# Two rounds of graph layers: when a gather may start, and how the node numbers are multiplied

## The chip, the cores and the metric

The kernel runs on one core of a Trainium2 chip. The metric is the device time of one launch in microseconds (us). Before the change it is 2184.74 us, the median of 9 runs (2181.94 to 2186.77).

## The reference, cut to what matters

Two graph layers run one after the other over the same 6,250 nodes of 256 numbers and 106,250 edges (100,000 edges and a loop at each node), which come sorted by target node.

```python
# layer 0: a message network of one of two kinds on every edge, then a cell and three products a node
S = feat[src]
for r in range(2):
    msgs = where(rel == r, edge_nn(S, W_rel[r], b_rel[r]), msgs)
agg = segment_sum(msgs, dst, n_nodes)
gates = agg @ W_ih.T + b_ih + b_hh            # i, f, g, o
hn = sigmoid(o) * tanh(sigmoid(i) * tanh(g))
x = layernorm(x + mlp3(hn))
# layer 1: attention with 4 heads of 64
h = (x @ W).reshape(n, 4, 64)
e = leaky_relu(a_src[src] + a_dst[dst], 0.2)  # one logit an edge and head
ex = exp(e - segment_max(e, dst)[dst])
out = segment_sum(h[src] * ex / segment_sum(ex, dst)[dst], dst)
x = layernorm(x + relu(layernorm(out + x) * gamma + beta))
```

## The kernel before, in words

The edges are cut into 782 tiles of 128 (`TC`), seven tiles make a window (`WT`), two windows a group; there are 56 groups (`NG`) in pairs, the last four alone. The kernel runs in four stretches.

**Start, to about 212 us.** The edge list is packed, and TensorE makes both kinds of message for all nodes (L1557, L1571) and stores them as table `parts`. Sixty gathers of the first layer (L1605) are issued in it already; the list `soon` holds their tiles.

**First aggregation, about 212 to 1160 us.** A loop over n from 60 to 785 is written out by hand. Step n issues one gather of 128 message rows from the table by an indirect DMA of the POOL queue (L1717), and adds the tile that was gathered four steps earlier (`LAG`) to its group's sum on TensorE (L2175, `sum0`). For every four finished groups a chain `update` is started, which a small hand scheduler (`Steps`) moves on a little at each step: gates (L2006), small products (L2030 to L2054), norm, turn (L2079), product with the attention weights (L2092), store of the new rows. For the first 12 windows the 60 early tiles are summed by extra chains (`sums_ahead`).

**Second aggregation, about 1160 to 2133 us.** Step t issues the gather of 128 rows of the new table (L1717, the same helper line). Four steps later its logits count as landed; when the last tile of a window counts as landed, ScalarE copies that window's logits out of the rows (L2626), and at the first tile of the next group that tile's logits (L2618). Then `weights` makes the weights of a whole pair (L2378 to L2409), `weighted` multiplies the rows by them on VectorE (L2424 to L2430), and `sum1` sums them on TensorE (L2546). `finish` ends a group. Meanwhile `ahead` brings, for a later pair, the slot of each edge's target within its group: it loads 15 tiles' slots, the same for all 128 partitions, as `dB` (L2313), compares them with the partition number to a one-hot `ohT` (L2338) and multiplies it with the group's node numbers `node3` (L2345). The `dB` tile has one buffer.

**End, 2133 to 2183.6 us.** The last weights, sums and norms, without gathers.

The gathers of both aggregations land in a ring of ten windows' buffers. On the POOL queue they stand one behind the other. What holds a gather back is its buffer, the landing of the gather eight before it, and a tie that `Pace.hold` adds: `passes` notes at the end of each step the last VectorE instruction issued so far, and gather n waits for the one noted `ahead` steps earlier. `AHEAD0` is 14 in the first aggregation; in the second it is `AHEAD1` = 8 and a surplus that falls from 42 to 0 over 252 steps and rises again over the last 42.

Three classes of tiles within a group matter for the change: tiles 0 to 6 of a group point at its lower 64 node slots, tiles 10 to 14 at its upper 64, tiles 7 to 9 at all 128 (`MID` = 7, 10; `LOW` = 64; `GS` = 15).

Of the kernel before, what the change touches and what calls it, by code (L numbers as in the profile page):

```python
# [38 lines left out]
ET = mybir.EngineType  # L39
# [3 lines left out]
P = 128  # L43
N = 6250
D = 256
E = 106250
H = 4
# [18 lines left out]
WT = 7  # L66
# [18 lines left out]
AHEAD_G = range(AHEAD_W // 2)  # L85
LATE = 3
CR = 16 * WT
AHEAD0 = 2 * WT
AHEAD1 = WT + 1
NOROW = NP + P // 2 - 1  # L90
SORTED = "the fast path runs only where the chip has found the edges sorted"

# [1547 lines left out]
def fast(  # L1640
# [46 lines left out]
    def at(ap, offset, dims):  # L1687
        return bass.AP(tensor=ap.tensor, offset=ap.offset + offset, ap=dims)
# [35 lines left out]
    class Steps:  # L1724
# [18 lines left out]
        def finish(self):  # L1743
            while self.chains:
                self.step()

    class Pace:
# [4 lines left out]

        def passes(self):
            traced = nc.cur_bb.bb.instructions
            self.passed.append(next(i for i in reversed(traced) if i.engine == ET.DVE))

        def hold(self, move, n, ahead):
            n -= self.first + ahead
            if n < 0:
                return  # L1760
            tc.add_manual_dep(
                move.ins,
                self.passed[n].name,
                mybir.DependencyInfo(mybir.DependencyClass.Sync, mybir.DependencyReason.DATA),
                reason="rows come no sooner than they are wanted",
            )
# [489 lines left out]
    with (  # L2256
# [45 lines left out]
        def ahead(pair, box):  # L2302

            cut = ring(ep, [P, P + 1], F32, "cut", 3)
            of = ring(ep, [P, 2 * GS, 2 * H], F32, "of", 3)
            box.update(cut=cut, of=of)
            i0, n = pair[0] % 2, len(pair)
            if i0 == 0:
                box["dB"] = ring(ep, [P, 2, GS * P], BF16, "dB", 1)
            else:  # L2310
                box["dB"] = boxes[pair[0] - 1]["dB"]
            dB = box["dB"][:, i0 : i0 + n, :]
            nc.sync.dma_start(  # L2313
                dB.rearrange("p i e -> p (i e)"),
                at(slots, pair[0] * GS * P, [[0, P], [1, n * GS * P]]),
            )
            if pair in pairs[:2]:
                for i, g in enumerate(pair):
                    nc.sync.dma_start(
                        cut[i * GS * H : (i + 1) * GS * H, :],  # L2320
                        at(cuts, tiles_in(g)[0][0] * P, [[P, GS], [0, H], [1, P + 1]]),
                    )
            else:
                o = pair[0] % 2 * GS * H
                n = ((len(pair) - 1) * GS + len(tiles_in(pair[-1])[1])) * H
                pc = ring(tps, [P, P + 1], F32, "turn", 2)
                nc.tensor.matmul(
                    pc[:n, :],
                    pick[:, pair[0] % 8 // 2, o : o + n],
                    cut_all[:, pair[0] // 8, :],  # L2330
                    start=True,
                    stop=True,
                )
                nc.scalar.copy(cut[:n, :], pc[:n, :])
            yield 12 if len(pair) > 1 else 8
            for i, g in enumerate(pair):
                ohT = ring(ep, [P, GS, P], BF16, "ohT", 2)
                nc.vector.tensor_scalar(  # L2338
                    ohT.rearrange("p j e -> p (j e)"), dB[:, i, :], iota_p, None, op0=OP.is_equal
                )  # L2340
                yield 2
                n = len(tiles_in(g)[1])
                pn = ring(ops, [P, GS, 3, 2 * H], F32, "pn", 2)
                for j in range(n):
                    nc.tensor.matmul(  # L2345
                        pn[:, j, :, :].rearrange("p c a -> p (c a)"),
                        ohT[:, j, :],
                        node3[:, g, :, :].rearrange("p c a -> p (c a)"),
                        start=True,
                        stop=True,  # L2350
                    )
                    if j == WT:
                        yield 1
                yield 1
                nc.vector.tensor_reduce(
                    of[:, i * GS : i * GS + n, :],
                    pn[:, :n, :, :].rearrange("p j c a -> p j a c"),
                    axis=AX.X,
                    op=OP.add,
                )  # L2360
                yield 1
# [56 lines left out]
        def weighted(g, w, o, n, of, ex, top):  # L2418

            if g not in ohs:  # L2420
                ohs[g] = ring(ep, [P, (2 * WT - 2) * LOW + 3 * P], F32, "oh1", 2)
                one_hot(ohs[g], g, slot, MID[1])
            gw = ring(ep, [P, WT if n > 1 else 1, D + 2 * H], F32, f"gw{min(n, 2)}", 4)[:, :n, :]
            nc.vector.tensor_mul(  # L2424
                gw[:, :, HA:],
                top[:, o : o + n, :],
                first[:, WT * w : WT * w + n, None].to_broadcast([P, n, H]),
            )
            nc.scalar.copy(gw[:, :, D:HA], ex[:, o : o + n, :])  # L2429
            nc.vector.tensor_mul(  # L2430
                gw[:, :, :D].rearrange("p j (h f) -> p j h f", h=H),
                of[:, :n, :D].rearrange("p j (h f) -> p j h f", h=H),
                ex[:, o : o + n, :, None].to_broadcast([P, n, H, F]),
            )
            return gw

        def finish(g, ps):
# [76 lines left out]
        results = {}  # L2514

        def sum1():

            while late and len(queue) < 8:
                piece = late.pop(0)
                g, w, o, n = piece[:4]  # L2520
                gw = weighted(*piece)
                queue.extend((g, WT * w + j, gw[:, j, :]) for j in range(n))
            if not queue:
                return
            g, t, gw = queue[0]
            if g not in sums and g >= 2 and g - 2 not in read:
                return
            queue.pop(0)
            if g not in sums:
                sums[g] = ring(eps, [P, D + 2 * H], F32, "fps1", 2)  # L2530
                left[g] = len(tiles_in(g)[1])
                u = everyone
                if g % 2 == 0:
                    k3s[g // 2] = ring(fp, [P, 2, 3, D], F32, "k3", 2)
                of = k3s[g // 2].rearrange("p i c f -> p i (c f)")
                if len(pair_of[g]) == 1:
                    nc.sync.dma_start(of[:, g % 2, :], kept[g // 2, :, g % 2, :])
                elif g % 2 == 0:
                    nc.sync.dma_start(of, kept[g // 2])
            begins = left[g] == len(tiles_in(g)[1])  # L2540
            left[g] -= 1
            j = t - 2 * WT * g
            to, cols = place(j, MID[1])
            ohj = ohs[g][:, cols]
            ends = left[g] == 0 or j in (WT - 1, TC - 1 - 2 * WT * g)
            nc.tensor.matmul(sums[g][to, :], ohj, gw, start=begins, stop=ends)  # L2546
            if left[g] == 0:
                run.start(finish(g, sums[g]), 1)

        def aheads():  # L2550
            for pair in pairs:
# [42 lines left out]
        while t < TC + LAG or late or queue or run.chains:  # L2594
            if EARLY <= t < TC:
                w = t // WT
                if t % WT == 0:
                    G[w] = ring(rowsp, [P, WT * HA], F32, "G", 10).rearrange(
                        "p (j f) -> p j f", f=HA
                    )  # L2600
                move = gather(G[w][:, t - WT * w, :], rows1, idx1[:, t : t + 1])
                pace.hold(move, t, AHEAD1 + max(0, 6 * WT - (t - EARLY) // 6, 3 * WT - (TC - t) // 2))
            k = t - LAG
            if 0 <= k < TC:
# [6 lines left out]
                if k % (2 * WT) == 0:  # L2611
                    if g == pair[0]:
                        box["e"] = ring(ep, [P, 2 * GS, H], F32, "e", 3)
                    if g:
# [5 lines left out]
                        )  # L2620
                        if old is not pair:
                            run.start(weights(old, ob))
                if k == tiles_of(w)[0][-1]:
                    o = pair.index(g) * GS + WT * (w % 2)
                    own = len(tiles_of(w)[0])
                    nc.scalar.copy(box["e"][:, o : o + own, :], G[w][:, :own, D:HA])  # L2626
                    if w == NW - 1:
                        run.start(weights(pair, box))
            sum1()
# [67 lines left out]
```

## Time and profile before

| what | value |
|---|---|
| median of 9 runs | 2184.74 us (2181.94 to 2186.77) |
| profiled execution | 2185.4 us, span 2183.6 us |
| granted TensorE clock, mean | 0.839 |
| busy: PE, DVE, ACT, POOL | 73%, 60%, 23%, 71% |
| gathers of both aggregations on POOL (L1717) | 722, 21 early ones of the second, 761 |
| DMA queues | POOL's 33.7% of 16 engines' span, SP's 17.6% |

PE is TensorE, DVE VectorE, ACT ScalarE, POOL GpSimd, SP the queue that issues most plain DMAs. The span is the time from the first to the last recorded instruction; 1.8 us of the profiled execution lie around it. A row of the timeline view gives start, duration, engine, line, operation, output<-input, and in brackets the idle time before it with what ended that. Lines are those of the kernel before.

### The profile page before, as it was taken

To read this page: it belongs to the slowest core of one execution; us is meant where nothing else is said; L and a number is where in the kernel's file an instruction comes from. 1 tells how busy PE (TensorE), PEld (TensorE's weight loads), DVE (VectorE), ACT (ScalarE), POOL (GpSimd) and SP (SyncE) were. 2 spreads that over 40 slices of the span, in tenths; PEclk is the share of its full clock that TensorE was granted. 3 is DMA by queue.
4 is the path that set the end of the run, shared out by engine and by line. 5 is a ranking of instruction groups with operands and counts; after the bars stand their busy time and mean duration, and the time that the engine had idled before them with its cause. 6 is when DMAs were issued, how large, how long until landed. Compare 5 with 4: busy or idle time off the path is not lost.

```text
span 2183.6 us, 23269 instructions
## 1 busy us (share of the span) xinstructions
PE 1588.6 (73%) x6390; PEld 851.8 (39%) x6390; DVE 1320.0 (60%) x3622; ACT 498.7 (23%) x1538; POOL 1548.9 (71%) x1610
## 2 busy tenths in 40 slices
PE   8988998788888898888995656565565556555564
PEld 5656544333333343333554333233232333333332
DVE  7854344434333433434443788888877777878786
ACT  3333032122211222122342121221211112121112
POOL 2465677777777777777777777777777777777770
PEclk9999999999989989999997777676776767677776
DMA  5356645445554555445555555555555555554551
GB/s 158 113 170 175 187 147 185 145 141 171 167 161 127 165 167 166 131 154 172 184 156 166 173 177 161 165 168 159 178 164 159 164 159 164 159 173 150 171 153 37
DMA packets 146105, 346.12 MB, mean 159 GB/s; under 512 B 36154, under 2 KB 66720, under 8 KB 145965
## 3 DMA queue, kind: packets, MB, share of 16 engines
q0 software_dynamic: 76048, 207.99, 33.7%
q1 hardware_dynamic: 67741, 133.51, 17.6%
q10 hardware_dynamic: 2176, 3.05, 0.4%
q8 instruction: 52, 0.85, 0.2%
q14 instruction: 88, 0.72, 0.1%
HBM read 291.90 MB, written 52.52 MB: 158 GB/s over the span
## 4 chain that ended last, share of the span: by engine, by line
PE 29%; DVE 23%; DMA 17%; issue 11%; POOL 7%; ACT 5%; DVEq 0%; SPq 0%; ACTq 0%; POOLq 0%
PE fps L2175 11%; DMA G<-parts,fidx 8%; DMA G<-rows,fidx 8%; POOL G L1717 7%; DVE gw L2430 6%; PE fpg L2006 5%; PE fps L2546 4%; DVE oh L1832 4%; PE fpg L2092 2%; PE fps L2288 1%; PE fpm L1571 1%; DVE fst L2476 1%; ACT fy L2484 1%; PE fpg L2054 1%; DVE ohT L2338 1%
## 5 line engine op out<-in xcount | busy, mean ns | idle before, releaser
L1717 POOL DMA_INDIRECT G<-rows,fidx x761 | 732.7, 963 | 232.0 <-issue 132.0
L1717 POOL DMA_INDIRECT G<-parts,fidx x722 | 694.3, 962 | 231.1 <-issue 154.0
L2546 PE MATMUL fps<-gw,oh 128*64 128x264 f32 (+1 forms) x1674 | 465.3, 466 | 187.9 <-DVE gw L2430 187.9
L2175 PE MATMUL fps<-G,oh 128*64 128x257 f32 (+1 forms) x1674 | 501.8, 418 | 114.9 <-DMA G<-parts,fidx 101.2
L2546 PEld LDWEIGHTS fps<-gw,oh 128*64 128x64 f32 (+1 forms) x1674 | 240.3, 176 | 332.9 <-DVE gw L2430 202.5
L2175 PEld LDWEIGHTS fps<-G,oh 128*64 128x64 f32 (+1 forms) x1674 | 210.2, 156 | 382.1 <-DMA G<-parts,fidx 181.7
L2430 DVE TENSOR_TENSOR gw<-G,bank 128x1792 f32<-128x1792 f32 (+1 forms) x167 | 249.0, 1491 | 58.0 <-ACT gw L2429 57.9
L2006 PE MATMUL fpg<-faT,fWihT 128*128 128x512 f32 (+2 forms) x432 | 171.7, 522 | 0.0
L1832 DVE TENSOR_TENSOR oh<-bank,fslot 128x448 f32<-128x448 f32 (+2 forms) x318 | 156.6, 548 | 9.4 <-ACT bank L2409 6.6
L1924 DVE TENSOR_SCALAR kind<-fps 128x1 f32<-128x1 f32 x112 | 12.5, 153 | 213.5 <-PE fps L2175 213.5
L1571 PE MATMUL fpm<-fWrT,fhT 128*128 128x256 f32 x392 | 96.5, 400 | 14.0 <-DVE fms L1579 14.0
L2126 DVE COPY nd<-hr 128x4 f32<-128x4 f32 x53 | 10.0, 189 | 156.0 <-ACT hr L2098 156.0
L2006 PEld LDWEIGHTS fpg<-faT,fWihT 128*128 128x128 f32 x432 | 72.1, 193 | 67.1 <-issue 56.2
L1557 PE MATMUL fph<-fxc,fWrT 128*128 128x512 f32 (+1 forms) x208 | 89.9, 582 | 4.8 <-DMA fWrT<-in_WrT_dram 4.8
L1605 POOL DMA_INDIRECT G<-parts,fidx x60 | 62.2, 1036 | 42.0 <-DVE fms L1579 18.0
L1571 PEld LDWEIGHTS fpm<-fWrT,fhT 128*128 128x128 f32 x392 | 76.9, 200 | 32.7 <-DVE fms L1579 11.2
L2345 PE MATMUL pn<-node,ohT 128*128 128x24 bf16 x837 | 41.0, 180 | 66.2 <-DVE ohT L2338 66.2
L2484 ACT ACTIVATE fy<-fy,frs 128x256 f32<-128x256 f32 x112 | 66.9, 597 | 87.3 <-DVE frs L2481 87.0
L2478 ACT ACTIVATE frs<-fmv,eps_c 128x1 f32<-128x1 f32 x112 | 32.9, 294 | 228.6 <-DVE gw L2424 150.8
L2378 PE MATMUL turn<-fident,e 128*120 128x128 f32 (+2 forms) x30 | 11.8, 393 | 98.3 <-ACT e L2618 98.3
L2092 PE MATMUL fpg<-Wx,fyT 128*128 128x264 f32 x224 | 74.8, 463 | 3.0 <-ACT fyT L2083 3.0
L2345 PEld LDWEIGHTS <-ohT 128*128 128x128 bf16 x837 | 34.2, 103 | 107.2 <-DVE ohT L2338 74.1
(348 smaller groups left out, 1970.1 us busy)
## 6 DMA issues: line engine op xcount, KB each, us to landing
dB<-slots SPq DMA_DIRECT2D x26, 960.0 KB, 5.5
kept<-keep SPq DMA_DIRECT2D x26, 768.0 KB, 4.6
k<-kept SPq DMA_DIRECT2D x26, 768.0 KB
loop<-parts SPq DMA_DIRECT2D x55, 256.0 KB, 2.8
parts<-fms SPq DMA_DIRECT2D x49, 256.0 KB, 2.6
G<-parts,fidx POOLq DMA_INDIRECT x782
G<-rows,fidx POOLq DMA_INDIRECT x761
out_dram<-fy SPq DMA_DIRECT2D x56, 128.0 KB, 1.9
```

Of the source, the lines that this page charges most:

```text
L1557: nc.tensor.matmul(ph[:, :cols], WrT_s[:, r, k, m * P : (m + 1) * P], xc[:, k, :cols], start=(k == 0), stop=(k == 1),)
L1571: made = nc.tensor.matmul(pm[:, r, :], hT[:, r, k, j * P : (j + 1) * P], WrT_s[:, r, k, :], start=(k == 0), stop=(k == 1),)
L1605: nc.gpsimd.indirect_dma_start(out=of[:, n % WT, :D], out_offset=None, in_=parts0[: 2 * P * block, :], in_offset=bass.IndirectOffsetOnAxis ...
L1717: return nc.gpsimd.indirect_dma_start(out=to_tile, out_offset=None, in_=table, in_offset=bass.IndirectOffsetOnAxis(ap=idx, axis=0),)
L1832: nc.vector.tensor_tensor(to[:, o : o + len(js) * n].rearrange("p (j s) -> p j s", s=n), iota_s[:, None, cols].to_broadcast([P, len(js), n ...
L2006: nc.tensor.matmul(pg[:, :cols], WihT_s[:, k, c * P : (c + 1) * P], aT[:, k, :cols], start=(k == 0), stop=(k == 1),)
L2092: nc.tensor.matmul(ph[u, :], hs[i][:, k, u], Wx[:, k, :], start=(k == 0), stop=(k == 1))
L2175: nc.tensor.matmul(sums[g][to, :], ohj, got[t], start=begins, stop=ends)
L2345: nc.tensor.matmul(pn[:, j, :, :].rearrange("p c a -> p (c a)"), ohT[:, j, :], node3[:, g, :, :].rearrange("p c a -> p (c a)"), start=True ...
L2430: nc.vector.tensor_mul(gw[:, :, :D].rearrange("p j (h f) -> p j h f", h=H), of[:, :n, :D].rearrange("p j (h f) -> p j h f", h=H), ex[:, o ...
L2484: nc.scalar.activation(y, y, AF.Identity, bias=m, scale=r)
L2546: nc.tensor.matmul(sums[g][to, :], ohj, gw, start=begins, stop=ends)
```

## The change

Ties: a gather is now held only where its number divides by four (`EVERY`), so one wait stands ahead of four gathers; it is 6 steps back in the first aggregation and 4 (with the same surplus) in the second, in place of 14 and 8; and what is noted at the end of a step is TensorE's last instruction, not VectorE's.

Node-number products: a tile of the lower half and one of the upper half now share one product. The slots of tile j are loaded to the lower 64 partitions and those of tile j+10 to the upper 64, so `dB` and `ohT` have 10 tiles in place of 15; the node numbers are put by two ScalarE copies into `node2`, whose two halves hold the lower and the upper nodes and zeros elsewhere; 10 products replace 15. Three DMAs replace one. Five memsets are added once.

Logit copies: the copies of a group's two windows are made together, when its second window counts as landed.

The product of rows and weights (L2430) no longer waits for the gathers of its rows, since its weights come from their logits.

```diff
-AHEAD0 = 2 * WT
-AHEAD1 = WT + 1
+AHEAD0 = WT - 1
+AHEAD1 = WT - 3
+EVERY = 4
...
-            self.passed.append(next(i for i in reversed(traced) if i.engine == ET.DVE))
+            self.passed.append(next(i for i in reversed(traced) if i.engine == ET.PE))
 
         def hold(self, move, n, ahead):
+            if n % EVERY:
+                return
             n -= self.first + ahead
...
-                box["dB"] = ring(ep, [P, 2, GS * P], BF16, "dB", 1)
+                box["dB"] = ring(ep, [P, 2, MID[1] * P], BF16, "dB", 1)
...
-            nc.sync.dma_start(
-                dB.rearrange("p i e -> p (i e)"),
-                at(slots, pair[0] * GS * P, [[0, P], [1, n * GS * P]]),
-            )
+            for ps, c0, j0, jn in (
+                (low_s, 0, 0, MID[1]),
+                (high_s, 0, MID[1], GS - MID[1]),
+                (high_s, MID[0], MID[0], MID[1] - MID[0]),
+            ):
+                nc.sync.dma_start(
+                    dB[ps, :, c0 * P : (c0 + jn) * P],
+                    at(slots, (pair[0] * GS + j0) * P, [[0, LOW], [GS * P, n], [1, jn * P]]),
+                )
...
+                halves = node2[g % 4]
+                for h, ps in enumerate((low_s, high_s)):
+                    nc.scalar.copy(
+                        halves[ps, h, :], node3[ps, g, :, :].rearrange("p c a -> p (c a)")
+                    )
-                ohT = ring(ep, [P, GS, P], BF16, "ohT", 2)
+                ohT = ring(ep, [P, MID[1], P], BF16, "ohT", 2)
...
-                for j in range(n):
-                    nc.tensor.matmul(
-                        pn[:, j, :, :].rearrange("p c a -> p (c a)"),
-                        ohT[:, j, :],
-                        node3[:, g, :, :].rearrange("p c a -> p (c a)"),
-                        start=True,
-                        stop=True,
-                    )
+                for j in range(MID[1]):
+                    if j < GS - MID[1]:
+                        to, of_n = po[:, j : MID[1] + j + 1 : MID[1], :], halves
+                    elif j < MID[0]:
+                        to, of_n = po[:, j, :], halves[:, 0, :]
+                    else:
+                        to, of_n = po[:, j, :], node3[:, g, :, :].rearrange("p c a -> p (c a)")
+                    nc.tensor.matmul(to, ohT[:, j, :], of_n, start=True, stop=True)
...
+            for move in brought.get(w, [])[:n]:
+                tc.declare_no_dep(
+                    made.ins, move.ins, reason="the weights come from logits of these rows"
+                )
...
+        for halves in node2:
+            nc.vector.memset(halves, 0.0)
+        nc.vector.memset(ring(ep, [P, 2, MID[1] * P], BF16, "dB", 1), -1.0)
...
-                if k == tiles_of(w)[0][-1]:
-                    ...
-                    nc.scalar.copy(box["e"][:, o : o + own, :], G[w][:, :own, D:HA])
+                if k == tiles_of(w)[0][-1] and (w % 2 or w == NW - 1):
+                    for v in (w, w - 1) if w % 2 else (w,):
+                        ...
+                        nc.scalar.copy(box["e"][:, o : o + own, :], G[v][:, :own, D:HA])
```

More of the change, by code (lines that the diff above doesn't have):

```diff
@@ L2343, in ahead @@
                 pn = ring(ops, [P, GS, 3, 2 * H], F32, "pn", 2)
-                for j in range(n):
-                    nc.tensor.matmul(
-                        pn[:, j, :, :].rearrange("p c a -> p (c a)"),
-                        ohT[:, j, :],
-                        node3[:, g, :, :].rearrange("p c a -> p (c a)"),
-                        start=True,
-                        stop=True,
-                    )
-                    if j == WT:
+                po = pn.rearrange("p j c a -> p j (c a)")
+                for j in range(MID[1]):
[6 more added lines that the diff above has]
+                    nc.tensor.matmul(to, ohT[:, j, :], of_n, start=True, stop=True)
+                    if j == MID[1] // 2:
                         yield 1
@@ L2429, in weighted @@
             nc.scalar.copy(gw[:, :, D:HA], ex[:, o : o + n, :])
-            nc.vector.tensor_mul(
+            made = nc.vector.tensor_mul(
                 gw[:, :, :D].rearrange("p j (h f) -> p j h f", h=H),
@@ L2513, in fast @@
         sums, queue, read, ohs, k3s, left, written = {}, [], set(), {}, {}, {}, []
-        results = {}
+        results, brought = {}, {}
         def sum1():
@@ L2548, in sum1 @@
                 run.start(finish(g, sums[g]), 1)
+        node2 = [ep.tile([P, 2, 6 * H], BF16, name=f"node2_{i}") for i in range(4)]
+        for halves in node2:
+            nc.vector.memset(halves, 0.0)
+        nc.vector.memset(ring(ep, [P, 2, MID[1] * P], BF16, "dB", 1), -1.0)
         def aheads():
@@ L2601, in fast @@
                 move = gather(G[w][:, t - WT * w, :], rows1, idx1[:, t : t + 1])
+                brought.setdefault(w, []).append(move)
                 pace.hold(move, t, AHEAD1 + max(0, 6 * WT - (t - EARLY) // 6, 3 * WT - (TC - t) // 2))
@@ L2622, in fast @@
                             run.start(weights(old, ob))
-                if k == tiles_of(w)[0][-1]:
-                    o = pair.index(g) * GS + WT * (w % 2)
-                    own = len(tiles_of(w)[0])
-                    nc.scalar.copy(box["e"][:, o : o + own, :], G[w][:, :own, D:HA])
+                if k == tiles_of(w)[0][-1] and (w % 2 or w == NW - 1):
+                    for v in (w, w - 1) if w % 2 else (w,):
+                        o = pair.index(g) * GS + WT * (v % 2)
+                        own = len(tiles_of(v)[0])
+                        nc.scalar.copy(box["e"][:, o : o + own, :], G[v][:, :own, D:HA])
                     if w == NW - 1:
```

## The prediction, made before the changed kernel ran

> **What bounds the kernel now.** I read the page's slices first, then the costliest groups, then the timeline of single engines.
>
> ```profile
> PE   8988998788888898888995656565565556555564
> POOL 2465677777777777777777777777777777777770
> ```
>
> POOL's busy share is flat from the fifth slice to the last but one, while TensorE's falls from nine tenths to half in the second aggregation. A flat engine at seven tenths can be a full one whose gaps are its own; the group rows say so:
>
> ```profile
> L1717 POOL DMA_INDIRECT G<-rows,fidx x761 | 732.7, 963 | 232.0 <-issue 132.0
> L1717 POOL DMA_INDIRECT G<-parts,fidx x722 | 694.3, 962 | 231.1 <-issue 154.0
> ```
>
> A gather takes 0.96 us and has 0.31 us of gap ahead of it, most of it put down to no wait. The timeline of POOL shows the beat and one of the few breaks:
>
> ```profile
> 239.75 0.95 POOL L1717 DMA_INDIRECT G<-parts,fidx  x1 [3.96 <-PE fps L2175]
> 241.01 0.95 POOL L1717 DMA_INDIRECT G<-parts,fidx  x1 [0.30 <-issue]
> ...
> 268.77 0.95 POOL L1717 DMA_INDIRECT G<-parts,fidx  x1 [0.30 <-issue]
> ```
>
> From 241 to 2131 us a gather starts every 1.25 us (0.95 + 0.30), with one more break, of 4.56 us at 1157.9, where the last new rows are stored. In the waits of POOL no other of its gathers waits more than 0.8 us. So the time is: when the beat begins, the number of gathers, each gather's length, breaks, and 50 us of tail. TensorE, VectorE and ScalarE count only through these.
>
> **The change part by part.** Faster and slower mean over 0.2% (4.4 us), about what a measurement of this kernel can tell from none.
>
> *Ties to TensorE, first aggregation: the main term.* What stands behind a held gather on POOL is all later gathers, so each us it waits is a us of the end. By the program's order, the gather at 268.77 is number 100; it is now tied to the last TensorE instruction of step 94, the last gate product (L2006) of the first quad. TensorE's timeline:
>
> ```profile
> 255.17 3.78 PE L2175 MATMUL fps<-G,oh 128*128 128x257 f32 x18
> 258.88 1.98 PE L2006 MATMUL fpg<-faT,fWihT 128*128 128x512 f32 x4
> 260.79 3.16 PE L2175 MATMUL fps<-G,oh 128*64 128x257 f32 x12
> ...
> 276.37 1.98 PE L2006 MATMUL fpg<-faT,fWihT 128*128 128x512 f32 x4
> 278.28 4.08 PE L2175 MATMUL fps<-G,oh 128*64 128x257 f32 x20
> ```
>
> TensorE is busy without a pause here (40.00 of 40 us from 240 to 280, clock 1.00): it still sums the 60 early tiles, far behind the gathers. The tie's product ends at 276.37 + 1.98 = 278.35. From such an end to the gather's start I take 0.27 us: the matmul that released the gather at 239.75 ended at 239.48. So number 100 starts at 278.62 in place of 268.77: **+9.85 us**. I laid every held gather beside the end of its tied product; this is the deepest. Earlier ones lack 2.3 us (234.84; swallowed by the break at 239.75), 2.3 (248.69), 4.2, 7.7 and 8.8 (263.75); these are steps on the way to 9.85, not additions. The next lacks 5.9 and then 1.9, which the 9.85 covers. TensorE doesn't starve meanwhile: step 94 needs gather 90, issued ten before.
>
> Is the 9.85 given back? At the end of this stretch TensorE waits for landings: the chain shows the last gather, issued at 1134.26, landing 4.26 us later, and the sum (L2175) starting at 1138.56 with its idle time put down to that landing. The break at 1157.9 hangs from there, through the last update and its store. So all of it moves along, and the tail too.
>
> *Other ties.* From 340 to 1008 us products end 1.9 to 9.4 us ahead of the tied gathers. Two places are thin. At 1019.04 the tied sum ends 0.06 us ahead, 0.2 less than the wake needs. In the second aggregation the least is at 1490.80, where the surplus of steps has run out: the tied node-number product ends 0.4 us late, its neighbours 1.1 to 3 us early. There VectorE is the pacer behind TensorE (216.14 busy of 260 us from 1240 to 1500) and gets 14 one-hots shortened by 0.24 us each (below), 3.4 us. I take +0.2 for both, at most +3 each.
>
> *One wait for four gathers.* Gap with a tie 0.30 us; without any, at the early second-layer gathers (L1717, `idx_e`, 1138 to 1157 us) 0.30 as well. Worth 0.
>
> *Smaller one-hot.* A gather that starts while `ohT` (L2338) runs is longer:
>
> ```profile
> 1753.18 0.42 DVE L2468 TENSOR_TENSOR fy<-fy,k 128x256 f32<-128x256 f32 x1
> 1753.52 0.71 DVE L2338 TENSOR_SCALAR ohT<-dB,fiota_p 128x1920 bf16<-128x1920 bf16 x1
> 1753.82 1.24 POOL L1717 DMA_INDIRECT G<-rows,fidx  x1 [0.30 <-issue]
> ```
>
> The one-hot ends 0.41 us into the gather, which takes 1.24 for 0.95: 0.13 us less than what was left of the one-hot. Other such gathers fit the same: 0.62 left, 0.50 longer; 0.17 left, 0.04. After 1240 us 28 gathers are longer so, by 6.1 us in all. Ten tiles for fifteen make 0.716 x 10/15 = 0.48 us, 0.24 less. With the phases kept, each loses up to 0.24: -5.2 us. But 19 one-hots that now start with the gather and cost nothing would start 0.24 earlier and leave 0.22, 0.09 each: +1.7. A one-hot at a random moment gives nearly the same: 56 x 0.35 x 0.35 / 2 / 1.25 = 2.7 us in place of 6.1. I take **-3.5**, from -6 to 0.
>
> The Trainium skill (SBUF — State Buffer, "SBUF: two separate sides") says that VectorE in a two-port mode and GpSimd hold a shared pair of ports as an exclusive lock for the whole instruction. The stretched gather agrees; a one-hot that starts within a 0.95 us gather would by that rule wait for its end, but here it took at most 0.94 for 0.72. By the rule alone, at random moments, 56 x 0.72 x 0.72 / 2 / 1.25 = 11.5 us would become 5.2, and the sum +3.7 in place of +6.5.
>
> *Work that lies beside the beat.* TensorE: 277 node-number products fewer (837 to 560) at 0.18 us, 50 us by the row's mean, in a stretch where it is 55% busy and no one waits for it on POOL: 0. ScalarE: 112 more small copies at about 0.21 us (L2626's mean), 23 us over 950 where it is 20% busy: 0. SP: 60 more issues at 0.33 us; `dB` is asked for 12 steps (15 us) ahead and lands in 5.5 us: 0, and if it came later, TensorE's lead over the tied gathers, 5 to 13 us through most of that stretch, covers it. Logit copies: they idle 154.6 us on landings, once a window; now once a group. Who waits for L2626 is POOL, 0.3 us: 0; at the very end one more copy, +0.2 at most. L2430's dropped waits: its idle time of 58.0 us is put down to ScalarE's copy (57.9), none to a DMA: 0. Memsets: at 1165, where VectorE waits 6.8 us for a load: 0. If one of these covers failed, VectorE would fall behind and the price is the thin ties' above.
>
> **Sum.** +9.85 + 0.2 - 3.5 = +6.5 on the profiled 2185.4 (span 2183.6 and 1.8 around it): 2191.9. That execution lies 0.7 above the median of the runs; on the median, 2184.7 + 6.5 = **2191.2**, +0.3%.
>
> **The rivals.** (1) *The delay is not paid, and the kernel is faster.* One mechanism: TensorE's backlog at gather 100 is smaller than the trace gives, since its ends are modelled, or the break of 4.56 us takes it up. Price: without the tie's term 2184.7 - 5.2 = 2179.5. It decides where the backlog at 268.77 is under about 1 us, not 9.6; between, up to 8, the time is the same. Against it: 40 us without a pause on TensorE, and a landing, not TensorE, at the end of the stretch. (2) *Further ties bind.* The thin ones at 1019 and 1490 give 3 us each, as VectorE or TensorE slips by what lies between neighbouring ties (1 to 3 us), and the one-hots' phases give nothing back: 2184.7 + 9.85 + 6 = 2200.5. For it: no slack there; against it: less work on both engines. (3) *The change doesn't do what it says:* the ties hold nothing and the products save time that no one waits for: 2184.7. For it: two of the four parts are just that. Against it: the list of late products.
>
> **How the numbers follow.** Forecast 0.60, with its own range 2187 to 2196 (tie 8 to 12, for a clock of TensorE that differs by a few per cent over the 55 us; stretch -6 to 0); 0.10 of it lies within 4.4 us. Rival 1: 0.15, of which 0.11 faster and 0.04 the same. Rival 2: 0.19, slower. Rival 3: 0.06, the same. So faster 0.11, same 0.20, slower 0.69. The range takes in most of rival 2 and the nearer half of rival 1: 2182 to 2199.
>
> **What the profile after would show.** Right: a break before POOL's gathers between 245 and 280 us, summing to about 10 us, put down to TensorE (L2175, L2006); the beat of 1.25 us after it; the last gather some 6 us later than 2131; `ohT` at 0.48 us and stretched gathers of at most 1.2 us; the tail unchanged. Wrong: no breaks there; breaks of POOL in the second aggregation above 1 us; a beat below 1.25; or a last gather no later than now.

## The result, and the profile after

The changed kernel takes 2195.66 us, the median of 11 runs (2190.43 to 2197.36), beside 2185.26 us for the kernel before in the same series (33 runs, 2180.21 to 2193.14). The ratio is 1.0046, with a 95% interval of 1.0037 to 1.0054: 10.4 us slower (8.1 to 11.8), where +6.5 was predicted. The profiled execution took 2193.41 us, 2.2 less than that median; its span is 2191.6 us, 8.0 more than before, at a granted clock of 0.84.

The slices and the groups of gathers look as before: POOL is flat at seven tenths, a gather takes 0.96 us. (A row of a group gives, behind the count, us busy in all and mean ns of one, then us idle ahead of them and what ended most of it.)

```profile
PE   8988998888878887889986565565564646555564
POOL 2465577777777777777776777777777777777770
...
L1718 POOL DMA_INDIRECT G<-rows,fidx x761 | 734.3, 965 | 232.0 <-issue 210.2
L1718 POOL DMA_INDIRECT G<-parts,fidx x722 | 693.7, 961 | 240.0 <-issue 182.7
```

Only the idle time ahead of the 722 gathers of the first aggregation grew, from 231.1 to 240.0 us. The timeline of POOL says where (in brackets the idle time ahead; 0.30 is the beat):

```profile
238.53 0.94 POOL L1718 DMA_INDIRECT G<-parts,fidx  x1 [1.37 <-PE fps L2178]
239.78 0.94 POOL L1718 DMA_INDIRECT G<-parts,fidx  x1 [0.30 <-issue]
241.02 0.95 POOL L1718 DMA_INDIRECT G<-parts,fidx  x1 [0.30 <-issue]
243.14 0.94 POOL L1718 DMA_INDIRECT G<-parts,fidx  x1 [1.17 <-PE fps L2178]
...
250.06 0.94 POOL L1718 DMA_INDIRECT G<-parts,fidx  x1 [2.23 <-PE fps L2178]
...
258.46 0.96 POOL L1718 DMA_INDIRECT G<-parts,fidx  x1 [3.70 <-PE fps L2178]
...
265.51 0.94 POOL L1718 DMA_INDIRECT G<-parts,fidx  x1 [2.29 <-PE fpg L2009]
...
271.54 0.94 POOL L1718 DMA_INDIRECT G<-parts,fidx  x1 [1.12 <-PE fpg L2009]
...
277.39 0.94 POOL L1718 DMA_INDIRECT G<-parts,fidx  x1 [0.93 <-PE fpg L2009]
...
1026.36 0.94 POOL L1718 DMA_INDIRECT G<-parts,fidx  x1 [0.65 <-PE fps L2178]
...
1171.72 1.00 POOL L2109 DMA_INDIRECT rows<-rows_l,tail_i  x1 [6.45 <-ACT keep L2102]
...
1494.55 0.94 POOL L1718 DMA_INDIRECT G<-rows,fidx  x1 [0.52 <-PE pn L2365]
...
2141.84 0.95 POOL L1718 DMA_INDIRECT G<-rows,fidx  x1 [0.31 <-issue]
```

The same gathers before the change, where the prediction does not show them:

```profile
1019.04 0.94 POOL L1717 DMA_INDIRECT G<-parts,fidx  x1 [0.30 <-issue]
...
1485.75 0.95 POOL L1717 DMA_INDIRECT G<-rows,fidx  x1 [0.30 <-DVE fy L2488]
...
2131.01 0.98 POOL L1717 DMA_INDIRECT G<-rows,fidx  x1 [0.30 <-issue]
```

Every fourth gather from 243.14 to 277.39 waits for TensorE. Less the beat's 0.305 each, these six waits sum to 0.86 + 1.92 + 3.39 + 1.99 + 0.82 + 0.62 = 9.6 us. TensorE's timeline shows the gate products (L2009, L2006 before) that release the last three:

```profile
263.36 1.88 PE L2009 MATMUL fpg<-faT,fWihT 128*128 128x512 f32 x4
...
269.39 1.88 PE L2009 MATMUL fpg<-faT,fWihT 128*128 128x512 f32 x4
...
275.14 1.98 PE L2009 MATMUL fpg<-faT,fWihT 128*128 128x512 f32 x4
```

They end at 265.24, 271.27 and 277.12; each gather starts 0.27 us later, the wake that the prediction took. The same gathers in both profiled executions, by the start of each:

| gather | before | after | later by |
|---|---|---|---|
| end of the early break | 239.75 | 238.53 | -1.22 |
| number 100, end of the first ties | 268.77 | 277.39 | 8.62 |
| the first thin tie | 1019.04 | 1026.36 | 7.32 |
| the last of the 21 early ones, just after the pause between the aggregations | 1166.34 | 1175.55 | 9.21 |
| number 272 of the second aggregation, held by its tie after | 1485.75 | 1494.55 | 8.80 |
| number 276, which the prediction named as thin | 1490.80 | 1499.71 | 8.91 |
| the last | 2131.01 | 2141.84 | 10.83 |
| end of the span | 2183.6 | 2191.6 | 8.0 |

### The profile page after: what moved, and what is told of

Its sections match the earlier page's. It is cut to its first block, busy times and chain, and to the rows that moved or that the text cites. A ratio compares the mean times of both kernels' runs of the same rounds, so it can differ in the third digit from the quotient of the medians.

```text
span 2191.6 us, 21850 instructions
## 1 busy us (share of the span) xinstructions
PE 1588.8 (72%) x6113; PEld 847.8 (39%) x6113; DVE 1311.6 (60%) x3627; ACT 512.9 (23%) x1650; POOL 1548.6 (71%) x1610
## 4 chain that ended last, share of the span: by engine, by line
PE 30%; DVE 25%; POOL 12%; DMA 12%; issue 9%; ACT 4%; SPq 0%; ACTq 0%; DVEq 0%; POOLq 0%
POOL G L1718 12%; PE fps L2178 10%; DMA G<-parts,fidx 8%; DVE gw L2444 8%; PE fpg L2009 6%; PE fps L2564 6%; DVE oh L1835 4%; DMA G<-rows,fidx 2%; PE fpg L2095 2%; PE fps L2291 1%; DVE fst L2494 1%; DVE ohT L2351 1%; PE fpm L1572 1%; ACT fy L2502 1%; DVE fy L2482 1%
## 5 line engine op out<-in xcount | busy, mean ns | idle before, releaser
L2444 DVE TENSOR_TENSOR gw<-G,bank 128x1792 f32<-128x1792 f32 (+1 forms) x167 | 248.9, 1490 | 58.4 <-ACT gw L2443 55.0
L2009 PE MATMUL fpg<-faT,fWihT 128*128 128x512 f32 (+2 forms) x432 | 172.5, 524 | 0.0
L1835 DVE TENSOR_TENSOR oh<-bank,fslot 128x448 f32<-128x448 f32 (+2 forms) x318 | 156.6, 548 | 10.2 <-ACT bank L2423 7.4
L2009 PEld LDWEIGHTS fpg<-faT,fWihT 128*128 128x128 f32 x432 | 72.9, 195 | 67.1 <-issue 56.2
L2365 PE MATMUL pn<-node,ohT 128*128 128x24 bf16 (+1 forms) x560 | 35.5, 191 | 69.6 <-DVE ohT L2351 65.9
L2365 PEld LDWEIGHTS <-ohT 128*128 128x128 bf16 x560 | 28.4, 107 | 110.5 <-DVE ohT L2351 77.0
```

Source lines behind the costliest of these rows:

```text
L1835: nc.vector.tensor_tensor(to[:, o : o + len(js) * n].rearrange("p (j s) -> p j s", s=n), iota_s[:, None, cols].to_broadcast([P, len(js), n ...
L2009: nc.tensor.matmul(pg[:, :cols], WihT_s[:, k, c * P : (c + 1) * P], aT[:, k, :cols], start=(k == 0), stop=(k == 1),)
L2365: nc.tensor.matmul(to, ohT[:, j, :], of_n, start=True, stop=True)
L2444: made = nc.vector.tensor_mul(gw[:, :, :D].rearrange("p j (h f) -> p j h f", h=H), of[:, :n, :D].rearrange("p j (h f) -> p j h f", h=H), e ...
```

## The experiments

Two theories stood. *The ties' wait*: the loss is the six waits above, and the other parts of the change are worth little. *The products*: the ties' wait is given back somewhere, and the smaller one-hot, the three loads in place of one or the grouped copies make the difference. A second question came up in the trace: the smaller one-hot was to lengthen fewer gathers, and did not. By "lengthening" I mean the sum of what gathers take beyond 0.948 us, about their usual time. It is a net sum: gathers below 0.948 us count against it.

The first four kernels ran on a chip on which the kernel before itself takes 2762.47 us, and g1 to g3 on another on which it takes 2735.62; they come last. f1 to f4 ran where it takes 2182.39 us (23 runs, 2179.17 to 2186.94), h1 where it takes 2182.20.

### f1: the new ties alone

The kernel before with the new ties and nothing else.

```diff
-AHEAD0 = 2 * WT
-AHEAD1 = WT + 1
+AHEAD0 = WT - 1
+AHEAD1 = WT - 3
+EVERY = 4
...
-            ... if i.engine == ET.DVE))
+            ... if i.engine == ET.PE))
...
+            if n % EVERY:
+                return
```

> The kernel before with the ties alone changed, again; the first four runs came from a chip on which the kernel before itself took 2762 us and this one 5% less, so they say nothing of the 2185 us at issue. On a chip that runs the kernel before in about 2185 us: theory A (TensorE's backlog at the first ties is the whole loss) 2195, breaks of 9 to 10.5 us between 240 and 285 us; theory B (shared with the products and copies) 2190. Where the kernel before takes about 2760 again: 2636 as measured there.

Measured: 2196.20 us (2192.35 to 2198.91), ratio 1.0066 [1.0053, 1.0079], +13.8 us. The breaks from 243 to 278 us sum to 9.6 again. The two thin ties take 1.56 and 1.03 us, where the changed kernel has 0.35 and 0.21. That the smaller products make this difference is not shown: the first of the two ties lies ahead of every node-number product (the first starts at 1198 us), and up to there both kernels give TensorE the same work. The waits of POOL name the tie:

```profile
POOL G L1718 <- PE fps L2178: 23.1, 42, 3.7
```

The columns are us in total, times, longest. The ties alone lose all that the change loses, and by the medians 3.4 us more; the intervals (11.6 to 17.2 here, 8.1 to 11.8 for the change, on another chip) just meet, so whether the other parts give something back beside the new ties stays open.

### f2: all but the ties

```diff
-AHEAD0 = WT - 1
-AHEAD1 = WT - 3
-EVERY = 4
+AHEAD0 = 2 * WT
+AHEAD1 = WT + 1
+EVERY = 1
...
-            ... if i.engine == ET.PE))
+            ... if i.engine == ET.DVE))
```

> The changed kernel with the ties of before, again. Where the kernel before takes about 2185 us: theory A 2182 (the prediction's -3.5 for the smaller one-hot) to 2187 (gathers stretched as in the changed kernel's profile), and no break after 240 us; theory B 2189 to 2191. Where it takes about 2760: 2742 as measured.

Measured: 2183.42 us (2178.79 to 2186.09), ratio 1.0002 [0.9993, 1.0010]. Products, loads and copies together change nothing that can be measured (-1.5 to +2.2 us). After 240 us no gather of the aggregations waits over 0.8 us in POOL's waits:

```profile
POOL G L1718 <- issue: 290.1, 952, 0.3
...
POOL G L1718 <- DMA G<-parts,fidx: 17.7, 48, 0.8
```

The lengthening in the second aggregation is 11.8 us, where the kernel before has 10.8. So the smaller one-hot does not lower it, with either kind of tie.

### f3: the same engine, farther back

The changed kernel with one number changed: ties to TensorE's last instruction, every fourth gather, but 14 steps back in the first aggregation in place of 6.

```diff
-AHEAD0 = WT - 1
+AHEAD0 = 2 * WT
```

> The changed kernel with 14 steps back in the first aggregation, again. Where the kernel before takes about 2185 us: theory A no break between 241 and 285 us and 9.6 us less than the changed kernel, 2185 to 2187; theory B 2190; theory C (the engine of the tie costs, not the steps) 2194 to 2196. Where it takes about 2760: 2622 as measured.

Measured: 2183.24 us (2180.82 to 2188.44), ratio 1.0011 [1.0001, 1.0021], +0.9 us. No break is left from 240 us to the pause, and the longest wait for a sum on TensorE is one of those before 240 us:

```profile
POOL G L1718 <- PE fps L2178: 13.6, 42, 1.1
```

So it is the six steps together with TensorE's backlog that cost, not the engine as such, nor one wait for four gathers. Whether six steps back to VectorE would cost as much was not run on a chip of the usual speed (e3 and g3 ran on others).

### f4: a one-hot that reads PSUM

To see whether the lengthening comes from the one-hot, it is made by an instruction that compares with the partition number in PSUM (`own_s`, a column more in the tile `bank`, filled once by ScalarE). The ties are those of before.

```diff
-                nc.vector.tensor_scalar(
-                    ohT.rearrange("p j e -> p (j e)"), dB[:, i, :], iota_p, None, op0=OP.is_equal
-                )
+                nc.vector.tensor_tensor(
+                    ohT.rearrange("p j e -> p (j e)"),
+                    dB[:, i, :],
+                    own_s.to_broadcast([P, MID[1] * P]),
+                    op=OP.is_equal,
+                )
```

> The changed kernel with the ties of before, and the one-hot made by a comparison of two tensors, one of them (the partition's number) in PSUM, as the group one-hots (L1835) are made, which never stretch a gather. VectorE's work on it rises from 0.55 to an estimated 1.6 us each (the 448-element form takes 0.55), 57 us in all, in a stretch where it is 79 to 83% busy. If a gather that starts within the one-hot is what is longer, no gather is stretched by it any more and the time falls by up to the 8.1 us that these made in the changed kernel, against the changed kernel with the old ties: 2177 to 2181 where the kernel before takes 2185. If the length of a gather has another cause: the same stretch under other names, 2185 to 2188. If VectorE becomes the bound instead: breaks of POOL in the second aggregation, over 2188.

Measured: 2193.49 us (2189.67 to 2194.94), ratio 1.0043 [1.0029, 1.0056], +11.1 us. The lengthening in the second aggregation fell from 11.8 to 1.2 us. But the new one-hot takes 1.48 us, 56 times 0.93 more than before, and VectorE became the engine that the ties wait for. Timelines of VectorE and POOL:

```profile
1405.15 2.02 DVE L2449 TENSOR_TENSOR gw<-G,bank 128x1792 f32<-128x1792 f32 x1 [0.15 <-ACT gw L2448]
1407.09 0.15 DVE L2504 SCALAR_TENSOR_TENSOR frs<-fmv,frs 128x1 f32<-128x1 f32 x1
```

```profile
1404.02 0.95 POOL L1718 DMA_INDIRECT G<-rows,fidx  x1 [0.30 <-issue]
1407.51 0.95 POOL L1718 DMA_INDIRECT G<-rows,fidx  x1 [2.54 <-DVE frs L2504]
```

The gather at 1407.51 waits for the last VectorE instruction of eight steps earlier. Such breaks between 1407 and 1511 us sum to 15.3 us, and eat the 10.6 that the shorter gathers gave. They do not make the whole loss: the span is 12.7 us longer than f2's, and 2.7 of it are longer gathers in the first aggregation, 1.7 the pause, 1.3 a later start and 1.9 the tail, which no run ties to the one-hot.

This one-hot differs in two things, the operand in PSUM and the instruction, which compares two tensors. The instruction alone does not spare a gather: in the changed kernel 11 gathers start within a product of two tensors that both lie in SBUF (`fhn`, L2029), and all are longer, 1.2 us on average; of 157 that start within the product of rows and weights, which reads `bank` in PSUM (L2444), one takes over 0.97. (Counted are gathers that start more than 0.09 us behind the instruction's start and 0.2 ahead of its end.)

### h1: the same one-hot with loose ties

f4 with the ties of the second aggregation 3 x 7 = 21 steps back (g1's expectation, below, names 18; its edit has 21), so that VectorE's lateness holds no gather.

```diff
-AHEAD1 = WT + 1
+AHEAD1 = 3 * WT
```

> The kernel of g1_psum_loose once more, to see it where the kernel before takes its usual 2182 to 2186 us and gathers follow each other without breaks (g1 ran where that kernel took 2735.62). First theory (the beat of the gathers is stretched only by VectorE instructions that lie in SBUF alone, and f4's loss came from the tie to a VectorE that the longer one-hot had made late): the gathers of the second aggregation are stretched by 1 to 3 us instead of 8.7 to 10.8, no break of the beat stands in 1400-1520 us, and the time is 6 to 9 us below the kernel before. Rival (VectorE itself, with 56 one-hots of 1.48 us instead of 0.55, sets the time there, tied or not): the time is at or above the kernel before, and the wait shows as breaks elsewhere or as a tail after the last gather longer than 51.6 us.

Measured: 2181.68 us (2178.50 to 2184.24, 11 runs) beside 2182.20 (2179.83 to 2186.80, 15 runs), ratio 0.9995 [0.9986, 1.0004]. Each theory held for one half. The beat did what the first said: no break in the second aggregation, lengthening 1.5 us in place of 11.8, the last gather at 2120.71 us, 9.1 earlier than in f2. The end did what the rival said: the tail after the last gather grew from 49.7 (f2) to 60.0 us. The timeline of POOL and VectorE shows both:

```profile
1383.36 0.95 POOL L1718 DMA_INDIRECT G<-rows,fidx  x1 [0.30 <-DVE fy L2490]
1383.38 1.48 DVE L2353 TENSOR_TENSOR ohT<-dB,bank 128x1280 bf16<-128x1280 bf16 x1
1384.61 0.95 POOL L1718 DMA_INDIRECT G<-rows,fidx  x1 [0.30 <-issue]
...
2120.71 0.94 POOL L1718 DMA_INDIRECT G<-rows,fidx  x1 [0.30 <-issue]
...
2158.94 2.02 DVE L2449 TENSOR_TENSOR gw<-G,bank 128x1792 f32<-128x1792 f32 x1 [0.15 <-ACT gw L2448]
```

The gather at 1384.61 starts inside the one-hot and is not lengthened. At the end, the last large product of weights and rows starts 38.2 us after the last gather; in f2 it starts at 2157.57, 27.7 us after. So VectorE comes to it 1.4 us later than in f2, though the rows are there 9.1 us earlier: in this execution VectorE's chain, not the beat, sets the end. The windows view gives its load (for 1500 to 1760 us: PE, PEld, DVE, ACT, POOL busy, clock, DMA share, GB/s):

```profile
1500.00:1760.00 260.00, 149.23 (x680) 84.41 (x676) 218.74 (x522) 56.66 (x254) 196.95 (x208) 0.76 0.58 155
```

VectorE is 84% busy there; in f2 it is 202.69 of 260 us, 78%. The two limits of the second aggregation, POOL's beat and VectorE's chain, lie so close that the 9 us taken from the one with 52 us more work on the other (56 times 0.93) come back at the end.

### e1 to e4 and g1 to g3: two chips on which the kernel before is slower

The edits are those of f1 (e1), f2 (e2), f3 (e4) and h1 (g1), and two more. In e3 and g3 the changed kernel's ties go to VectorE's last instruction:

```diff
-            ... if i.engine == ET.PE))
+            ... if i.engine == ET.DVE))
```

In g2 the first aggregation's gathers are not tied up to number 147:

```diff
-            if n % EVERY:
+            if n % EVERY or (self.first and n < 148):
```

> The kernel before with the ties alone changed (TensorE's last instruction, 6 and 4 steps back, every fourth gather). Theory A, the ties' wait on TensorE's backlog at the start of the first aggregation is the whole loss: breaks of 9 to 10.5 us in POOL's beat between 240 and 285 us as in the changed kernel (9.6 there), and 2185.3 + 9.9 = 2195 us, as slow as the whole change. Theory B, the loss is shared between the ties and something the products or copies cost (longer gathers, a later last row): about 2190, 4 to 6 us faster than the whole change.

> The changed kernel with the ties of before (VectorE's last instruction, 14 and 8 steps back, every gather): the paired products, the grouped logit copies and the dropped waits alone. Theory A: no break after 240 us, and what is left is the length of the gathers in the second aggregation. The prediction's own term would make it 2185.3 - 3.5 = 2182; the changed kernel's profile, where the shorter one-hot stretches 36 gathers by 8.1 us where the longer one stretched 30 by 6.3, makes it 2185 to 2188. Theory B: 2189 to 2191.

> The changed kernel with VectorE's last instruction noted in place of TensorE's, all else kept. By the trace of before, the deepest lateness is then 7.65 us (the gather at 263.75, tied to a product of the first gates on VectorE), as VectorE waits for TensorE there. Theory A: breaks of 7.5 to 9 us between 240 and 290 us and 1 to 2 us less time than with TensorE's tie, if the tie at 1490 us (1.8 us late by that trace) stays free, the same if it binds: 2193 to 2196. Theory C, the engine of the tie is what costs: no breaks, 2185 to 2187.

> The changed kernel with 14 steps in place of 6 in the first aggregation, still every fourth gather and TensorE's. By the trace of before, each tied product then ends at least 0.9 us ahead of its gather after 240 us. Theory A: no break there, 9.6 us less than the changed kernel, 2185 to 2187. Theory B, half of the loss lies elsewhere: 2190. Theory C: the engine costs, not the steps: 2194 to 2196.

> The products and the grouped copies are kept. The second aggregation's one-hot (ohT) is compared with a partition number that lies in PSUM, as in f4_onehot_psum, and its gathers are tied 18 steps back to VectorE's last instruction instead of 8, in every step. First theory (the beat of the gathers is stretched only by VectorE instructions that lie in SBUF alone, and f4's loss came from the tie to a VectorE that the longer one-hot had made late): the gathers of the second aggregation are stretched by 1 to 3 us instead of 8.7, no break of the beat stands in 1400-1520 us, and the time is 6 to 9 us below the kernel before (2173 to 2177 where that takes 2182.4). Rival (VectorE itself, with 56 one-hots of 1.48 us instead of 0.55, is what sets the time there, tied or not): the breaks go, but the time comes out at or above the kernel before, with the wait shown as a longer tail after the last gather.

> The changed kernel without the ties of the first aggregation's gathers up to no. 147 of the run (so that the first tied gather is no. 149 of the run or later); all other ties to TensorE's last instruction, every fourth, 6 and 4 steps back, stay. First theory (the loss is the wait of the first ties, 9.6 us of breaks between 240 and 290 us, and no other tie costs anything): no break of the beat in 240-290 us, at most 0.6 us of breaks at other ties apart from the pause between the aggregations (4.3 to 6.0 us), and a time of 2182 to 2186 us where the kernel before takes 2182.4 (+0 to +4). Rival (the ties cost throughout, and the first ones only delay what the later ones would have delayed anyway): breaks come up at the next ties, 300 to 345 us, and the time stays 8 us or more above the kernel before.

> The changed kernel with every fourth gather tied 6 and 4 steps back as it is, but to VectorE's last instruction, not TensorE's. First theory (what costs is the nearness of 6 steps: between 250 and 270 us both engines are behind, VectorE's tied instruction ends up to 7.65 us after the gather's start in the kernel before, TensorE's 9.58): breaks of 7.5 to 9 us in 240-290 us and a time 7 to 10 us above the kernel before, 1 to 2 us less than with TensorE's. Rival (the engine is what costs): no break over 1 us there, and the kernel before's time within 2 us.

| kernel | us | ratio to the kernel before there |
|---|---|---|
| e1, new ties alone | 2636.41 | 0.9525 [0.9494, 0.9556] |
| e2, all but the ties | 2742.29 | 0.9929 [0.9904, 0.9953] |
| e3, tied to VectorE | 2743.62 | 0.9928 [0.9905, 0.9951] |
| e4, 14 steps back | 2622.39 | 0.9487 [0.9460, 0.9515] |
| g1, one-hot in PSUM, loose ties | 2832.05 | 1.0362 [1.0325, 1.0399] |
| g2, first ties out | 2624.15 | 0.9611 [0.9582, 0.9639] |
| g3, tied to VectorE | 2704.07 | 0.9899 [0.9872, 0.9926] |

None of the expectations, written for the usual beat, was met in its numbers. There the beat does not hold: a gather still takes 0.95 us, but the idle time ahead of them is 398 to 587 us in each aggregation's group in place of some 230, spread over the whole aggregation. Group and waits of e2 and waits of g2:

```profile
L1718 POOL DMA_INDIRECT G<-rows,fidx x761 | 724.9, 953 | 505.8 <-issue 176.1
```

```profile
POOL G L1718 <- DVE gw L2444: 109.6, 28, 13.9
```

```profile
POOL G L1718 <- remote: 124.0, 46, 5.3
POOL G L1718 <- PE fps L2178: 95.2, 29, 51.9
```

("remote" is a wait whose release the trace does not hold.) One wait in g2 can be read: with the first ties gone, POOL runs ahead and waits 51.9 us at the first tie that is left, number 148 at 424 us. Its rival had expected such breaks at the next ties, but also a time 8 us or more above the kernel before, and it is 4% below. What the first ties cost or save there can't be told, since the changed kernel was not timed on these chips; on the usual chip f3 has no such break. What the table does show is an order: ties to TensorE give 4 to 5% there, ties to VectorE 1% or less, and g1, with the longer one-hot and looser ties, loses 3.6%. Why those chips are slower is not settled. Packets of the gathers take the same time (4,160-byte packets 0.25 us on average in e2 and in f2), VectorE's and POOL's instructions too, and TensorE's granted clock is 0.75 to 0.78 in place of 0.84; the rest of the difference lies in waits that the traces do not attribute. The nearest relatives of the changed kernel that ran there are e4 and g2.

## Why the prediction was right, point by point

| term | predicted | measured, profiled executions |
|---|---|---|
| first ties | +9.85 | +9.6 |
| thin ties | +0.2 | +0.56 (1.56 + 1.03 in f1) |
| smaller one-hot | -3.5 | +1.9 |
| pause between the aggregations | 0 | +1.9 |
| tail | 0 | -2.8 |
| other | 0 | -3.2 |
| sum | +6.5 | +8.0; by the medians +10.4 |

**The ties.** The mechanism, the place, the engine and the released instruction (the gate product) came out as worked out from the list of late products, and the price to 1.2 us; the small ones on the way were steps, not additions. In the prediction's own terms number 100 starts 8.62 us later, not 9.85: its product ends at 277.12 in place of 278.35, as the whole stretch begins 1.2 us earlier. Executions differ by as much there (number 100 stands at 266.84 to 269.10 in those with the old steps), and f1 against f2, on one chip, gives 10.2 (277.88 for 267.71). f1 and f3 show the cause: the ties alone bring the loss, and with 14 steps for 6 it is gone. The wake of 0.27 us held.

**Carried to the end.** The gathers are 8.6 us later at number 100 and 7.3 to 10.8 later all the way. Rival 1 (the delay is not paid) is out: TensorE's backlog was 9.6, and the pause took nothing up.

**Further ties (rival 2).** The first thin place was the right one. In the second aggregation it was the neighbour that bound, number 272, four gathers ahead of the one named, which waits for nothing after. The two cost 0.35 and 0.21 us, and 1.56 and 1.03 in f1: in sum 0.6 and 2.6, between the +0.2 that was taken and the 6 of rival 2. Why f1's are larger is not shown.

**Work beside the beat.** One wait for four gathers, 277 products fewer, 112 copies more and 60 loads more were put at nothing. f2, which has all but the first of these and the smaller one-hot, gives +1.0 us, with an interval from -1.5 to +2.2; f3, which has the one wait too, gives +0.9.

**The step that was mis-sized: the smaller one-hot.** Two things in it were wrong. It takes 0.547 us, not 0.48: of the 0.716 us only part goes with the number of tiles (0.716 - 0.547 = 0.169 for 640 of 1920 numbers; if time goes evenly with numbers, an estimate from these two sizes, 0.21 us are fixed). And the phases were not kept. In the trace after:

```profile
1774.20 0.55 DVE L2351 TENSOR_SCALAR ohT<-dB,fiota_p 128x1280 bf16<-128x1280 bf16 x1
1774.31 1.25 POOL L1718 DMA_INDIRECT G<-rows,fidx  x1 [0.30 <-issue]
```

The one-hot starts 0.11 us ahead of the gather and leaves 0.44, 0.30 of which the gather pays.

One-hot by one-hot, the two profiles show which part of the term failed. Before, 18 one-hots start 0.2 to 0.5 us ahead of a gather and cost it 4.9 us in all; the same ones cost 2.1 after, less, as was expected. But 17 start at most 0.083 us ahead before and cost nothing, while one that starts 0.089 ahead costs 0.50: a few hundredths of a us decide. The prediction let these start 0.24 us earlier, leave 0.22 and cost 0.09 each, +1.7 in all. On average they start only 0.07 us earlier, which takes nearly all of them over that edge, leave 0.42 and cost 4.2 in all. f2 and f3 have the same phases as the changed kernel, f1 those of before, so they go with the smaller products and not with the ties; why the start moves by 0.07 us is not shown.

In the second aggregation 36 gathers are lengthened by the one-hot for 8.1 us, where there were 30 for 6.3; all lengthening there is 12.7 for 10.8, and f2 and f3 agree (11.8 and 12.6). The net sum even hides a part: the usual gather is 0.949 us in the profile of before, 0.947 in f2 and 0.946 in the others. Counted from each profile's own usual time, the gathers after 1200 us are lengthened by 10.4 us before and 10.6 in f1, with the large one-hot, and by 14.6 in the changed kernel, 12.6 in f2 and 14.4 in f3, with the small one; f4 and h1 have 3.2 and 3.4. The estimate for random moments would have been 56 x 0.42 x 0.42 / 2 / 1.25 = 4.0 us in place of 2.7, and for the large one-hot 56 x 0.586 x 0.586 / 2 / 1.25 = 7.7, where 6.3 was measured: neither execution is random, and the sign could not be had from that.

**Pause and tail.** The pause ahead of the last store of rows was 4.56 us before and 6.45 after. It is not shown to be the ties': it is 4.55 in f2, 4.70 in f3, 5.18 in h1, 6.14 in f1 and 6.25 in f4, so both sizes come with the old ties. It scatters by some 2 us and the prediction had no range for that. The tail was 51.6 and is 48.8; f1 to f4 have 49.7 to 51.6. What the table calls other is 1.2 us by which the stretch of the first ties begins earlier (239.75 to 238.53), 1.5 by which the gathers from number 100 to the pause are shorter in all, and a rest. Those gathers are shorter because the usual one takes 0.946 us for 0.949, which no part of the change is shown to make. Tail and other take back what one-hot and pause added: that the sum was better than its terms is luck. Another 2.4 us of the 10.4 by the medians lie in executions that were not profiled.

**What the rule on the ports makes of it.** Row first: in the changed kernel, after 1200 us, 41 gathers start within a one-hot of 0.55 us and take 1.146 us on average, up to 1.26; in f4 and h1, in the same stretch, 113 gathers start within a one-hot of 1.48 us that reads PSUM, and none takes more than 0.955. (Two earlier ones take 1.13 and 1.14, but another VectorE instruction, L2287, starts 0.34 us into each.) The Trainium skill (SBUF — State Buffer, "SBUF: two separate sides") names who holds the pair of ports shared with GpSimd: a VectorE instruction in a two-port mode, or, against a GpSimd instruction that reads SBUF, one with two inputs in SBUF. That agrees, since the one-hot of f4 and h1 has one input in SBUF and runs at 1.16 ns for each number against 0.43. That whichever of the two starts first has the pair for its whole instruction does not show here: the gather is lengthened by 0.13 to 0.14 us less than is left of the one-hot, and not at all where the one-hot starts at most 0.083 us ahead (17 one-hots before, which take 0.756 us on average for 0.716); and a one-hot that starts within a gather is not held for its rest (0.77 us at most for 0.55).

## What to carry to other kernels

A tie holds a whole queue: lay each held instruction beside the end of what it is tied to in the trace of before, take the deepest lateness, not the sum, and look for the stretch in which that engine still works off an earlier backlog. A gain from where two engines' instructions happen to meet has no sign until the chain that sets their phase is known. And before taking time from the engine that sets the beat, look how far behind the next one is: in h1 the beat came out 9 us shorter for 52 us more work on VectorE, and the time stayed the same.

## What the runs showed of the hardware that was not expected

A gather is not lengthened by a VectorE instruction of 1.48 us that reads one operand from PSUM (0.955 us at most), and is by one of 0.55 us that doesn't (1.146 us on average). In the trace of before, a one-hot that starts 0.083 us ahead of a gather costs it nothing and one that starts 0.089 ahead costs 0.50 us. The same program takes 2182 us on some chips and 2736 to 2762 on others, with the durations of gathers and VectorE's instructions the same, and the order of kernels turns round between them: the new ties alone cost 0.7% on the one (f1) and give 4.8% on the other (e1). No version that ran beats the kernel before where that takes 2182 us; h1, f2 and f3 come within 0.2% of it.
